# Patch gather by one-hot matmuls: f32 tables with a ScalarE selection, against bf16 parts with a VectorE comparison

## The chip, the cores and the metric

The kernel runs on one core of a Trainium2 chip. A core has five engines that run side by side, each through its own list of instructions in order: TensorE (PE, matmuls; PEld is its weight load), VectorE (DVE), ScalarE (ACT), GpSimd (POOL, here mostly an issuer of DMAs, with a few memsets) and SyncE (SP, DMA issue only). An engine waits where an instruction needs something that another engine or a DMA has not delivered yet. The metric is the device time of the core in microseconds.

## The reference

The input x has 8 images of 32 channels with 128 x 128 pixels. What is computed (normalisations `_gn`, two layers with residuals):

```python
def _patch_match_stack(x):           # for each pixel: the 8 of 25 offsets with the lowest 3x3-patch distance
    for dy in range(-2, 3):
        for dx in range(-2, 3):
            d = ((x - shifted(x, dy, dx)) ** 2).sum(1, keepdims=True)
            costs.append(conv(d, ones3x3, pad=1))
    _, idx = top_k(-cost, 8)
    g = x[:, yy(idx), xx(idx)]       # gather of the 8 shifted copies
    return g                         # [B, 32*8, H, W]

xb = _patch_match_stack(gn(x))
dct = conv(xb, dct_w, groups=32)
h = relu(depthwise3x3(conv1x1(xb, w1), w2))
h = relu(depthwise3x3(conv1x1(h, w3), w4))
wiener = sigmoid(depthwise3x3(conv1x1(h, w5), w6))
x = x + conv1x1(conv(wiener * dct, inv_dct_w, groups=32), agg_w)
x = x + conv5x5(gn(x), k5)           # per channel
```

## The kernel before

**Work on an image ahead of its use.** While the convolutions of image b run, the next image is prepared in small tasks: statistics and normalisation (`prep`), then `sources` and `squares`, `costs`, `places`. `squares` makes the differences to shifted copies on DVE (L421), squares them on ACT (L429) and sums over channels on PE (L436). `costs` sums patches on DVE, transposes on PE and takes the best 8 of 25 with MAX8 and FIND_INDEX8 on DVE (L513, L514). `places` turns offset numbers into places in a source table, transposes them on PE, and stores them as bf16 through POOL to `idxd` in HBM (L549).

**The source table.** `sources` transposes the normalised image on PE, four rows at a time (L390), copies it out on ACT (L392) and stores it through POOL to `xl` (L394). From `xl`, eighteen DMAs on POOL (L402, L406) build `xtd`: for each image row, 16 shifts and 11 pieces of 12 pixels (TW = 12, NT = 11), the 32 channels of the pixel in f32. A piece of 12 output pixels with offsets from -2 to 2 reaches QW = 16 source pixels, and four output rows reach 8 source rows, so 8 x 16 = 128 table rows: one for each partition.

**The gather.** A unit is half of the offsets (4 of 8) of four image rows; a step of eight rows has four units. `gather_load` fetches the table (`xt`, for every second unit) and two index tiles `ib`, each a row of HBM copied to all 128 partitions (L582). `gather_select` makes the one-hot on ACT: Square(ib - partition) in L596, Relu(1 - that) in L597, into `sel` in f32. `gather_pixels` runs one f32 matmul for each piece and offset: 32 columns of weights from `xt`, 48 columns (4 rows x 12 pixels) of `sel`, into one of four column groups of PE (L611); each f32 matmul is two instructions. ACT copies the result to `xb` (L618), and POOL stores `xb` to HBM (L620) for the final stage, which loads it again as `xf` (L769).

**The convolutions.** Three stages i = 1, 2, 3 each have a 1x1 convolution and a 3x3 depthwise one. Half of the channels goes the v way: PE (L649), ACT copy to `tv` (L657), then nine taps: the first on ACT (L700), eight on DVE (L703, scalar_tensor_tensor over 1024 elements), activation on ACT (L707). The other half goes the t way: PE (L673), ACT copy (L680), two copies by SP's DMAs, depthwise as matmuls on PE (L729), activation on ACT (L742). The final stage multiplies by the DCT on PE and DVE (L788, L796) and projects (L809, L817).

**Order.** The lists of PE, DVE and ACT are in program order. The main loop runs over steps of eight rows, with substeps i = 3, 2, 1, 0; i = 0 is the final stage. In each substep stand: the v matmuls of stage i; the image tasks of queues P and Q; half of the selection of unit u + 1; the loads of unit u + 3; `tick`, which takes image tasks for DVE up to a credit (estimated costs, summed in `total`); the eight taps; the t matmuls; the gather matmuls of unit u; the depthwise matmuls of the substep before; the A tasks (ACT); the other half of the selection. Before the loop, a prologue fills four units; `until` runs turns of image tasks (up to 4 us of DVE work each) until the index rows that a load needs are there (`ready`). In a turn each queue's tasks run once, so a chain of tasks that changes queues takes several turns.

Of the kernel before, what the change touches and what calls it, by code (L numbers as in the profile page):

```python
# [15 lines left out]
P = 128  # L16
# [4 lines left out]
NS = H // R  # L21
TW = 12
NT = 11
QW = TW + 4
HR = 38
HX = W + 4
SR = 6
EPS = 1e-5


# [12 lines left out]
def bm3d_conv_preact(  # L43
# [89 lines left out]
    nc.vector.tensor_copy(neg[:, 28:32], cst[:, C_B + 24 : C_B + 24 + P : 32])  # L133
    nplace = const.tile([P, 1], F32, name="nplace")
    nc.vector.tensor_scalar(nplace, cst[:, C_Q : C_Q + 1], -1.0, None, op0=ALU.mult)

# [245 lines left out]
    def sources(b, xn):  # L382


        xl = dram.tile([H, W, C], F32, name=f"xl_{b}", tag="xl")
        for r in range(0, 32, 4):
            yield "P", 0
            pt = ps_x.tile([P, 4, P], F32, name=f"px_{b}_{r}", tag="x")
            for q in range(4):
                nc.tensor.transpose(pt[:, q], xn[:, 3 + r + q, 2 : 2 + W], ident)  # L390
            xs = work.tile([P, 4, P], F32, name=f"xs_{b}_{r}", tag="ct")
            nc.scalar.copy(xs, pt)  # L392
            for q in range(4):
                nc.gpsimd.dma_start(  # L394
                    xl.rearrange("(g r) x c -> r x g c", g=4)[r + q],
                    xs[:, q].rearrange("p (g c) -> p g c", c=C),
                )
        xt = xtd[b] = dram.tile([H, QW, NT, C], F32, name=f"xtd_{b}", tag="xtd")
        for j in range(QW):
            ta, tz = (1 if j < 2 else 0), (NT if j < 10 else NT - 1)  # L400
            xa = TW * ta + j - 2
            nc.gpsimd.dma_start(  # L402
                xt[:, j, ta:tz], xl[:, xa : xa + TW * (tz - ta - 1) + 1 : TW]
            )
        for ja, jz, t, at in ((0, 2, 0, 0), (10, QW, NT - 1, W - 1)):
            nc.gpsimd.dma_start(  # L406
                xt[:, ja:jz, t], xl[:, at : at + 1].to_broadcast([H, jz - ja, C])
            )

# [109 lines left out]
    def places(b, idx, i):  # L519


        if i == 0:
            idxd[b] = dram.tile([4, 8, K * 4, W], BF16, name=f"idxd_{b}", tag="idxd")
        yield "D", 2.6
# [8 lines left out]
        for lim in (10.0, 15.0, 20.0):  # L533
# [5 lines left out]
            o3,  # L539
            cst[:, C_BASE : C_BASE + 4].unsqueeze(1).to_broadcast([P, 64, 4]),  # L540
            ALU.add,
        )
        yield "P", 0
        for h in range(2):
            pt = ps_x.tile([P, 512], F32, name=f"pi_{b}_{i}_{h}", tag="x")
            nc.tensor.transpose(pt[:, :P], o[:, h * P : (h + 1) * P], ident)
            li = work.tile([P, P], BF16, name=f"li_{b}_{i}_{h}", tag="li")
            nc.scalar.copy(li, pt[:, :P])
            nc.gpsimd.dma_start(  # L549
                idxd[b][2 * h : 2 * h + 2, 2 * i : 2 * i + 2].rearrange("g s k x -> g (s k) x"),  # L550
                li,
            )
        ready.add((b, i))
        if i == 3:
            ready.add(b)

    ready = set()
    xbs, xts, ibs, selss = {}, {}, {}, {}

    def gather_load(b, s4, g):  # L560

        if g == 0:

            xt = xts[b, s4] = work.tile([P, NT, C], F32, name=f"xt_{b}_{s4}", tag="xt", bufs=3)
            ys = [min(max(4 * s4 - 2 + r, 0), H - 1) for r in range(8)]
            if ys[7] - ys[0] == 7:
                nc.gpsimd.dma_start(
                    xt.rearrange("p t c -> p (t c)"),
                    xtd[b][ys[0] : ys[0] + 8].rearrange("r x t c -> (r x) (t c)"),
                )  # L570
            else:
                for r, y in enumerate(ys):
                    nc.gpsimd.dma_start(
                        xt[QW * r : QW * (r + 1)].rearrange("p t c -> p (t c)"),
                        xtd[b][y].rearrange("x t c -> x (t c)"),
                    )
        for k2 in range(2):
            ib = work.tile(
                [P, 2, 4, W], BF16, name=f"ib_{b}_{s4}_{g}_{k2}", tag="ib", bufs=5
            )  # L580
            k0 = 4 * g + 2 * k2
            nc.gpsimd.dma_start(  # L582
                ib.rearrange("p k y x -> p (k y x)"),
                idxd[b][s4 // 8, s4 % 8, 4 * k0 : 4 * k0 + 8]
                .rearrange("k x -> (k x)")
                .partition_broadcast(P),
            )
            ibs[b, s4, g, k2] = ib

    def gather_select(b, s4, g, k2=(0, 1)):  # L590
        for k2 in k2:
            sel = work.tile(
                [P, 2, 4, W], F32, name=f"sel_{b}_{s4}_{g}_{k2}", tag="sel", bufs=4
            )
            ib = ibs.pop((b, s4, g, k2))
            nc.scalar.activation(ib, ib, AF.Square, bias=nplace)  # L596
            nc.scalar.activation(sel, ib, AF.Relu, scale=-1.0, bias=1.0)  # L597
            selss[b, s4, g, k2] = sel

    def gather_pixels(b, s4, g):  # L600

        n, h = s4 // 2, s4 % 2
        if h == 0 and g == 0:
            xbs[b, n] = xbp.tile([P, 2, R, W], F32, name=f"xb_{b}_{n}", tag="xb")
        xb, xt = xbs[b, n], xts[b, s4]
        sels = [selss.pop((b, s4, g, k2)) for k2 in range(2)]
        pg = ps_x.tile([P, 4, W], F32, name=f"pg_{b}_{s4}_{g}", tag="x")
        for t in range(NT):
            xa, xz = TW * t, min(TW * (t + 1), W)
            for j in range(4):  # L610
                nc.tensor.matmul(  # L611
                    pg[C * j : C * (j + 1), :, xa:xz],
                    xt[:, t],
                    sels[j // 2][:, j % 2, :, xa:xz],
                    start=True,
                    stop=True,
                )
        nc.scalar.copy(xb[:, g, 4 * h : 4 * h + 4], pg)  # L618
        if h == 1 and g == 1:
            nc.gpsimd.dma_start(xbd[b][:, :, R * n : R * (n + 1)], xb)  # L620
# [305 lines left out]
    def middle(b, mr):  # L926
# [40 lines left out]
    units = [  # L967
        (b, 2 * n + h, g) if n < NS else None
        for b, n in steps
        for h in range(2)  # L970
        for g in range(2)
    ]
# [3 lines left out]
    def unit(stage, u, *rest):  # L976
        if 0 <= u < len(units) and units[u]:
            if stage is gather_load:
                at = (units[u][0], units[u][1] % 8 // 2)
                until(lambda: at in ready, 4.0)  # L980
            stage(*units[u], *rest)
# [9 lines left out]

    total = 5.5 + 3.3 + 36 * 1.95 + 4 * 4.6 + 32 * 1.85 + 4 * 2.6 + 4 * 3.6 + 6.6
    owed = [0.0]
# [19 lines left out]
    with tc.manual_schedule(engines=ORDERED):  # L1013
# [19 lines left out]
        for s in range(len(steps) + 2):  # L1033
# [10 lines left out]
            for i in (3, 2, 1, 0):  # L1044
# [22 lines left out]
                if s < len(steps):  # L1067
                    unit(gather_select, u + 1, (0,))
                    unit(gather_load, u + 3)
# [11 lines left out]
                if s < len(steps):  # L1081
                    unit(gather_select, u + 1, (1,))
                    u += 1
# [72 lines left out]
```

## Time and profile before

| what | us |
|---|---|
| median of three runs | 6811.16 |
| lowest and highest of them | 6809.01, 6819.06 |
| span of the profiled execution, first to last instruction | 6807.3 |
| mean granted clock of PE in it | 0.973 |

Some more groups of the same execution (count, busy us in total, mean ns of one):

| group | count | busy | mean |
|---|---|---|---|
| PE pg L611, 128x48 f32 | 40960 | 559.6 | 208 |
| PE pw L729 | 31680 | 2144.1 | 422 |
| PE px L390, transposes | 256 | 41.1 | 283 |
| ACT t L680, copies of 512 | 768 | 414.6 | 579 |
| ACT acc L707, activations of 1024 | 384 | 406.9 | 1060 |
| ACT xs L392, copies of 512 | 64 | 36.6 | 571 |
| DVE df L421 | 576 | 532.5 | 976 |
| POOL ib L582, DMA issue | 1024 | 570.7 | 558 |
| POOL idxd L549, DMA issue | 64 | 52.1 | 818 |
| POOL xl L394, DMA issue | 256 | 193.9 | 764 |
| POOL xtd L402, DMA issue | 128 | 127.3 | 1005 |

Matmuls are pipelined, so the mean of one is longer than the distance from one start to the next; busy is the time in which at least one of the group ran. DMA queues moved 1021.41 MB. The first gather matmul starts at 142 us, the first tap of L703 at 209 us, the last gather matmul at 6630.7 us.

### The profile page before, as it was taken

The numbers are of one execution on the slowest core, as the hardware profiler recorded it, in microseconds if no ns is written. First come the engines' busy times: TensorE is split into PE (matmuls) and PEld (weight loads), VectorE is DVE, ScalarE is ACT, GpSimd is POOL, SyncE is SP. The second block draws the span as 40 slices with busy tenths as digits, with TensorE's granted clock in tenths as the row PEclk, the third lists the DMA queues.
The fourth block names the chain that finished last, engine by engine and source line by source line (L and its number), as shares of the span: only waits on it lengthen the run. The fifth ranks groups of instructions, "written<-read, shape, count | busy, mean of one in ns | idle before, by whom it ended". The sixth has DMA issues, their size and how long they took to land.

```text
span 6807.3 us, 257036 instructions
## 1 busy us (share of the span) xinstructions
PE 6354.3 (93%) x113378; PEld 3352.8 (49%) x113378; DVE 5860.4 (86%) x8822; ACT 5064.6 (74%) x6698; POOL 3246.7 (48%) x5351
## 2 busy tenths in 40 slices
PE   5798899999999999999999999999999999999997
PEld 1454454554545455454554455545555454455553
DVE  7789988989889898898988888899888899877776
ACT  5787778777687777877777777877769777687772
POOL 7354446444464444544445444454436554344334
PEclk8899999999999999999999999999999999999998
DMA  4566656666566675666756656566665666566653
GB/s 90 143 153 153 151 149 154 159 152 158 147 156 155 144 169 135 163 151 152 167 135 158 161 146 169 138 165 159 149 150 151 162 156 152 138 170 157 154 151 80
DMA packets 809627, 1021.41 MB, mean 150 GB/s; under 512 B 255456, under 2 KB 619936, under 8 KB 808512
## 3 DMA queue, kind: packets, MB, share of 16 engines
q0 software_dynamic: 422432, 745.61, 42.9%
q1 hardware_dynamic: 383568, 258.11, 17.4%
q8 instruction: 892, 14.61, 0.9%
q10 hardware_dynamic: 2512, 1.25, 0.1%
q14 instruction: 223, 1.83, 0.1%
HBM read 553.25 MB, written 217.01 MB: 113 GB/s over the span
## 4 chain that ended last, share of the span: by engine, by line
PE 55%; DVE 23%; ACT 8%; DMA 6%; issue 5%; POOL 3%; SPq 0%; ACTq 0%; DVEq 0%; POOLq 0%
PE pw L729 18%; DVE acc L703 15%; PE pv L649 13%; PE p L673 12%; PE pg L611 4%; DVE df L421 3%; PE pc L788 2%; DMA t<-t 2%; PE p L902 2%; ACT df L429 2%; ACT ib L596 2%; DVE idx L514 1%; PE pa L809 1%; DMA xf<-xbd 1%; DVE acc L796 1%
## 5 line engine op out<-in xcount | busy, mean ns | idle before, releaser
L703 DVE SCALAR_TENSOR_TENSOR acc<-tv,dwv,acc 128x1024 f32<-128x1024 f32 (+3 forms) x3264 | 4032.9, 1237 | 249.6 <-ACT acc L700 140.3
L729 PE MATMUL pw<-t,dwd 96*32 96x254 f32 (+7 forms) x31680 | 2144.1, 422 | 84.7 <-issue 40.5
L729 PEld LDWEIGHTS pw<-t,dwd 96*32 96x32 f32 (+1 forms) x31680 | 1103.9, 111 | 906.6 <-issue 440.7
L582 POOL DMA_DIRECT2D ib<-idxd x1024 | 570.7, 558 | 1796.5 <-ACT sel L597 1620.6
L596 ACT ACTIVATE ib<-ib,nplace 128x1024 bf16<-128x1024 bf16 x1024 | 1170.1, 1143 | 9.5 <-DMA ib<-idxd 9.5
L597 ACT ACTIVATE sel<-ib 128x1024 f32<-128x1024 bf16 x1024 | 1084.8, 1059 | 32.5
L673 PE MATMUL p<-acc,lw 128*32 128x256 f32 x16768 | 989.1, 381 | 25.3 <-ACT tv L657 22.7
L649 PE MATMUL pv<-acc,lw 128*128 128x512 f32 (+1 forms) x2112 | 980.7, 607 | 29.9 <-DVE acc L796 27.4
L769 POOL DMA_DIRECT2D xf<-xbd x1088 | 650.2, 630 | 304.2 <-PE pc L788 87.0
L673 PEld LDWEIGHTS p<-acc,lw 128*32 128x32 f32 x16768 | 556.2, 111 | 454.9 <-ACT tv L657 62.5
L657 ACT COPY tv<-pv 128x512 f32<-128x512 f32 (+2 forms) x784 | 438.1, 578 | 390.4 <-PE pv L649 374.2
L611 PEld LDWEIGHTS pg<-sel,xt 128*32 128x32 f32 x45056 | 575.5, 111 | 252.1 <-issue 54.2
L429 ACT ACTIVATE df<-df 128x786 f32<-128x786 f32 (+2 forms) x576 | 468.0, 859 | 291.9 <-DVE df L421 289.2
L611 PE MATMUL pg<-sel,xt 128*32 128x48 f32 x45056 | 592.7, 207 | 80.4 <-ACT sel L597 46.0
L421 DVE TENSOR_TENSOR df<-xn 128x786 f32<-128x786 f32 (+2 forms) x576 | 532.5, 976 | 116.0 <-PE pd L436 109.2
L742 ACT ACTIVATE acc<-pw 128x512 f32<-128x512 f32 (+2 forms) x808 | 439.9, 573 | 249.7 <-PE pw L729 249.0
L649 PEld LDWEIGHTS pv<-acc,lw 128*128 128x128 f32 x2112 | 384.2, 193 | 475.6 <-issue 398.1
L707 ACT ACTIVATE acc<-acc 128x1024 f32<-128x1024 f32 (+3 forms) x408 | 416.8, 1022 | 229.7 <-DVE acc L703 229.5
L680 ACT COPY t<-p 128x512 f32<-128x512 f32 x800 | 424.6, 570 | 127.7 <-PE p L673 125.7
L700 ACT ACTIVATE acc<-tv,dwv 128x1024 f32<-128x1024 f32 (+3 forms) x408 | 454.5, 1114 | 52.6 <-PE pa L809 35.0
L649 PE MATMUL pv<-xb,lw 128*128 128x512 f32 x1024 | 477.4, 609 | 0.0
L673 PE MATMUL p<-xb,lw 128*32 128x256 f32 x8192 | 468.1, 380 | 4.4 <-DVE xy L914 4.4
(151 smaller groups left out, 5782.5 us busy)
## 6 DMA issues: line engine op xcount, KB each, us to landing
ib<-idxd POOLq DMA_DIRECT2D x1024, 256.0 KB, 4.4
xbd<-xb POOLq DMA_DIRECT2D x128, 1024.0 KB, 6.7
xf<-xbd POOLq DMA_DIRECT2D x960, 128.0 KB, 7.3
t<-t SPq DMA_DIRECT2D x792, 128.0 KB
t<-t SPq DMA_DIRECT2D x384, 256.0 KB
tv<-tv SPq DMA_DIRECT2D x384, 130.0 KB
xt<-xtd POOLq DMA_DIRECT2D x240, 176.0 KB, 4.6
xl<-xs POOLq DMA_DIRECT2D x256, 64.0 KB, 2.6
```

Source lines behind the costliest of these rows:

```text
L421: nc.vector.tensor_sub(df[:, :, ca:cz], xn[:, r0 : r0 + SR, ca:cz], xn[:, r0 + dy : r0 + dy + SR, ca + dx : cz + dx],)
L429: nc.scalar.activation(df[:, :, ca:cz], df[:, :, ca:cz], AF.Square)
L582: nc.gpsimd.dma_start(ib.rearrange("p k y x -> p (k y x)"), idxd[b][s4 // 8, s4 % 8, 4 * k0 : 4 * k0 + 8] .rearrange("k x -> (k x)") .part ...
L596: nc.scalar.activation(ib, ib, AF.Square, bias=nplace)
L597: nc.scalar.activation(sel, ib, AF.Relu, scale=-1.0, bias=1.0)
L611: nc.tensor.matmul(pg[C * j : C * (j + 1), :, xa:xz], xt[:, t], sels[j // 2][:, j % 2, :, xa:xz], start=True, stop=True,)
L649: nc.tensor.matmul(ps[:, :hr], lhsT[:, g, P:CK], src(g)[:, h : h + hr], start=g == 0, stop=g == 1,)
L673: nc.tensor.matmul(ps[C * r : C * (r + 1), e, :nb], lhsT[:, g, s], rows[:, r : r + 4 * nb - 3 : 4], start=g == 0, stop=g == 1,)
L700: nc.scalar.activation(acc, rows, AF.Copy, scale=tap)
L703: nc.vector.scalar_tensor_tensor(acc, rows, tap, acc, op0=ALU.mult, op1=ALU.add)
L729: nc.tensor.matmul(pt[u][C * j : C * (j + 1), ka:kz, :nb, xa:xz], dwd[0:hi, i - 1, u, j, dx + 1], t[0:hi, j, ka:kz, :nb, xa + dx : xz + dx ...
L769: nc.gpsimd.dma_start(xf[p : p + C, m, j0:j1], src[g, m, (h + m + 1) % 2, :, :, ya:yz])
```

## The change

The table holds each pixel in three bf16 parts (the value rounded to bf16, the rest rounded, and the rest of that), 96 values in place of 32 f32. The parts are made from the normalised image: a copy to bf16 on ACT, a subtraction on DVE, again a copy and a subtraction; then each part is transposed as bf16. Three matmuls per piece and offset, one for each part, sum in PSUM. Pieces are 11 pixels, QW = 15, so 8 x 15 = 120 table rows; they start anew at column 64, six for each half. A unit is now all 8 offsets of four rows in one half of the columns, with one index tile of 2048 bf16. The one-hot is one comparison on DVE, in place, with the partition number. A matmul takes two offsets at once: 2 x 4 x 11 = 88 columns. `places` adds a base by half, and its result is stored in twice as many DMAs. A load also waits until the source table of its image is complete (`sourced`).

```diff
-TW = 12
-NT = 11
+TW = 11
+NT = 12
+HW = W // 2
+NP = 3
...
     def sources(b, xn):
-        xl = dram.tile([H, W, C], F32, name=f"xl_{b}", tag="xl")
+        xl = dram.tile([H, W, NP * C], BF16, name=f"xl_{b}", tag="xl")
         for r in range(0, 32, 4):
-            yield "P", 0
-            pt = ps_x.tile([P, 4, P], F32, name=f"px_{b}_{r}", tag="x")
-            for q in range(4):
-                nc.tensor.transpose(pt[:, q], xn[:, 3 + r + q, 2 : 2 + W], ident)
-            xs = work.tile([P, 4, P], F32, name=f"xs_{b}_{r}", tag="ct")
-            nc.scalar.copy(xs, pt)
-            for q in range(4):
+            rows = xn[:, 3 + r : 7 + r, 2 : 2 + W]
+            yield "A", 0
...
+            nc.scalar.copy(parts[0], rows)
+            yield "D", 0.7
+            nc.vector.tensor_sub(rest, rows, parts[0])
+            yield "A", 0
+            nc.scalar.copy(parts[1], rest)
+            yield "D", 0.7
+            nc.vector.tensor_sub(parts[2], rest, parts[1])
+            for q0 in (0, 2):
+                yield "P", 0
+                pt = ps_x.tile([P, 2, 4, NP, C], BF16, name=f"px_{b}_{r}_{q0}", tag="x")
+                for q in range(2):
+                    for s in range(NP):
+                        nc.tensor.transpose(pt[:, q, :, s], parts[s][:, q0 + q], ident_b)
+                xs = work.tile([P, 2, 4, NP * C], BF16, name=f"xs_{b}_{r}_{q0}", tag="xs")
+                nc.scalar.copy(xs, pt.rearrange("p q g s c -> p q g (s c)"))
+                for q in range(2):
+                    nc.gpsimd.dma_start(
+                        xl.rearrange("(g r) x e -> r x g e", g=4)[r + q0 + q], xs[:, q]
+                    )
+        xt = xtd[b] = dram.tile([H, QW, NT, NP * C], BF16, name=f"xtd_{b}", tag="xtd")
+        for j in range(QW):
+            for f in range(2):
...
                 nc.gpsimd.dma_start(
+                    xt[:, j, ta:tz], xl[:, xa : xa + TW * (tz - ta - 1) + 1 : TW]
+                )
...
+        sourced.add(b)
...
     def gather_load(b, s4, f):
...
-        for k2 in range(2):
-            ib = work.tile([P, 2, 4, W], BF16, name=f"ib_{b}_{s4}_{g}_{k2}", tag="ib", bufs=5)
...
+        ib = work.tile([P, K, 4, HW], BF16, name=f"ib_{b}_{s4}_{f}", tag="sel", bufs=4)
+        nc.gpsimd.dma_start(
+            ib.rearrange("p k y x -> p (k y x)"),
+            idxd[b][s4 % 8 // 2, s4 // 8 * 2 + s4 % 2, f].rearrange("k x -> (k x)").partition_broadcast(P),
+        )
...
-            nc.scalar.activation(ib, ib, AF.Square, bias=nplace)
-            nc.scalar.activation(sel, ib, AF.Relu, scale=-1.0, bias=1.0)
+    def gather_select(b, s4, f):
+        ib = ibs[b, s4, f]
+        nc.vector.tensor_scalar(ib, ib, place, None, op0=ALU.is_equal)
...
-        for t in range(NT):
-            xa, xz = TW * t, min(TW * (t + 1), W)
-            for j in range(4):
-                nc.tensor.matmul(
-                    pg[C * j : C * (j + 1), :, xa:xz],
-                    xt[:, t],
-                    sels[j // 2][:, j % 2, :, xa:xz],
-                    start=True,
-                    stop=True,
-                )
-        nc.scalar.copy(xb[:, g, 4 * h : 4 * h + 4], pg)
+        for t in range(NT // 2):
+            xa, xz = TW * t, min(TW * (t + 1), HW)
+            for s in range(NP):
+                for j in range(4):
+                    nc.tensor.matmul(
+                        pg[C * j : C * (j + 1), :, :, xa:xz],
+                        xt[: 8 * QW, f * (NT // 2) + t, C * s : C * (s + 1)],
+                        sel[: 8 * QW, j : j + 5 : 4, :, xa:xz],
+                        start=s == 0,
+                        stop=s == NP - 1,
+                        skip_group_check=True,
+                    )
+        nc.scalar.copy(xb[:, :, 4 * h : 4 * h + 4, HW * f : HW * (f + 1)], pg)
...
-                until(lambda: at in ready, 4.0)
+                until(lambda: at in ready and at[0] in sourced, 4.0)
...
-    total = 5.5 + 3.3 + 36 * 1.95 + 4 * 4.6 + 32 * 1.85 + 4 * 2.6 + 4 * 3.6 + 6.6
+    total = 5.5 + 3.3 + 8 * 1.4 + 36 * 1.95 + 4 * 4.6 + 32 * 1.85 + 4 * 2.6 + 4 * 3.6 + 6.6
...
-                    unit(gather_select, u + 1, (0,))
+                    unit(gather_select, u + 1)
                     unit(gather_load, u + 3)
                     tick(b, i)
...
-                    unit(gather_select, u + 1, (1,))
                     u += 1
```

## The prediction

> **What bounds the kernel now.** I read the engine totals first, then the engines' busy time by stretches of the span, then the groups of instructions by form, then the waits, and last the order in time of a few stretches.
>
> The engine totals give busy time and its share of the span: PE is nearly full, DVE is second.
>
> ```profile
> PE 6354.3 (93%) x113378; PEld 3352.8 (49%) x113378; DVE 5860.4 (86%) x8822; ACT 5064.6 (74%) x6698; POOL 3246.7 (48%) x5351
> ```
>
> The stretches (start:end, length, then busy us of PE, PEld, DVE, ACT, POOL) say where each is the limit.
>
> ```profile
> 0.00:210.00 210.00, 100.94 (x964) 38.14 (x968) 146.31 (x427) 109.19 (x153) 145.67 (x214) 0.76 0.44 98
> 210.00:580.00 370.00, 348.13 (x6398) 187.82 (x6390) 325.94 (x456) 304.03 (x399) 167.91 (x272) 0.98 0.62 154
> 580.00:830.00 250.00, 222.80 (x4120) 121.43 (x4122) 238.71 (x471) 186.76 (x246) 107.54 (x189) 0.97 0.63 148
> 830.00:5750.00 4920.00, 4690.63 (x84224) 2481.32 (x84220) 4337.01 (x6522) 3755.78 (x4973) 2400.79 (x3961) 0.98 0.63 154
> 5750.00:6650.00 900.00, 881.58 (x16448) 470.68 (x16444) 709.36 (x789) 673.17 (x868) 356.92 (x622) 0.99 0.61 153
> ```
>
> From 830 to 5750 us PE is busy 4691/4920 = 95.3%, DVE 88.2%. In the last image, where no next image is prepared, PE reaches 98.0% with DVE at 78.8%. From 580 to 830 us it is the other way round: DVE 95.5%, PE 89.1%, and there the chain of waits names DVE's taps (27%) first. So DVE's work is already a limit wherever it exceeds some 95% of the time.
>
> By form (count, busy us, mean ns of one):
>
> ```profile
> L703 DVE SCALAR_TENSOR_TENSOR acc<-tv,dwv,acc 128x1024 f32<-128x1024 f32 x3072 | 3940.6, 1284 | 232.4 <-ACT acc L700 130.7 <-PE p L673 4.6 <-DMA tv<-tv 0.9
> L596 ACT ACTIVATE ib<-ib,nplace 128x1024 bf16<-128x1024 bf16 x1024 | 1170.1, 1143 | 9.5 <-DMA ib<-idxd 9.5
> L597 ACT ACTIVATE sel<-ib 128x1024 f32<-128x1024 bf16 x1024 | 1084.8, 1059 | 32.5
> L796 DVE TENSOR_TENSOR acc<-acc,pc 128x512 f32<-128x512 f32 x496 | 308.5, 681 | 55.4 <-PE pc L788 55.4
> L532 DVE TENSOR_SCALAR oc<-oc 128x256 f32<-128x256 f32 x32 | 9.7, 302 | 1.1
> L367 DVE TENSOR_SCALAR xn<-xn,mr_a 128x5016 f32<-128x5016 f32 x8 | 23.6, 2952 | 0.4
> ```
>
> In time order, one gather unit and the depthwise matmuls behind it (start, length, tiles, count):
>
> ```profile
> 3035.49 1.09 PE L611 MATMUL pg<-sel,xt 128*32 128x48 f32 x88
> ...
> 3036.40 5.35 PE L729 MATMUL pw<-t,dwd 96*32 96x256 f32 x96
> ```
>
> **The change, part by part.**
>
> *ACT.* 1024 pairs of Square and Relu go: 1024 x (1.143 + 1.059) = 2255 us. Added are 128 copies of 512 elements (0.58 us, as the copies of L680) and 128 of 768 (0.8, between the 0.58 of 512 elements and L707's 1.06 of 1024) in place of 64 of 512 (0.57): 74 + 102 - 37 = +139. ACT falls from 5065 to about 2949 us, 43%. ACT was not the limit, so this pays only through waits: in 830 to 5750 us little of DVE's and PE's idle time names ACT's selection (PE at L611 about 25 us). I book nothing for it separately.
>
> *PE, the gather.* Before, a unit has 44 f32 matmuls, each issued as two instructions, hence 88 at 1.10/88 = 12.5 ns each, four column groups side by side. The depthwise row gives 5.35/96 = 55.7 ns for 256 columns. Slope: (55.7 - 12.5)/(256 - 48) = 0.208 ns a column, with 2.5 ns fixed. After, a unit has 6 x 3 x 4 = 72 bf16 instructions of 88 columns (72 in the last piece). No bf16 matmul is in the trace. Upper end: a column costs what it costs in an f32 pass, 2.5 + 88 x 0.208 = 20.8 ns, 1.50 us a unit. Lower end: columns cost nothing and only the 2.5 ns stay, 0.18 us. I take half the slope, because an f32 element has twice the bytes: 11.7 ns, 0.84 us. Then 512 x 0.26 = 133 us leave PE. The value is nearer to the 12.5 ns row than either end is. The Trainium skill (TensorE: Matmul & The Clock Gate, section Wait — 56ns, not 53.3ns?) puts a floor of about 25 ns under the start-to-start of small matmuls; by it a unit would take 72 x 25 = 1.80 us and PE would gain 358 us of work. The row above, 12.5 ns across four column groups, speaks against that floor here, and the measurement decides.
>
> *PE, the source transposes.* 256 instructions (0.66 us for four, 41 us in all) become 768 of bf16; at half the time each 61 us, at the same time each 123. I take +20. PE: 6354 - 133 + 20 = 6241 us.
>
> *DVE, the comparison.* 512 instructions of 2048 bf16 elements, in place. No bf16 instruction of DVE is in the trace. The two TENSOR_SCALAR rows give (2952 - 302)/(5016 - 256) = 0.557 ns an element, half of what the two-input rows take ((1284 - 681)/512 = 1.18). Either way two f32 inputs are read in some 1.1 to 1.2 ns, which I read as a limit by bytes. Upper end, f32 rate: 0.302 + 1792 x 0.557 = 1.30 us. Lower end: the 256-element row alone, 0.30 us. By bytes: 0.302 + 1792 x 0.279 = 0.80 us; less the overlap of neighbours I take 0.78, or 399 us in all. The Trainium skill (VectorE: DVE Perf Modes, section The perf-mode tier table) gives 693 ns for a bf16 tensor_scalar of 2048 elements in SBUF; by it the sum would be 355 us, and no row here shows it.
>
> *DVE, the split.* 128 subtractions of 512 elements at 0.68 (the L796 row): 87 us. DVE: 5860 + 399 + 87 = 6346 us, now above PE.
>
> *Order on DVE.* The comparison of the next unit stands ahead of the queued image work and of the eight taps. It waits for its index load, issued two units (some 24 us) earlier and landing in 4.4 us; ACT's idle time before the same data was 9.5 us in the whole run. So the wait costs nothing while the load keeps that lead; if POOL is late, the taps behind it are late, then ACT's activation and PE's next stage.
>
> *POOL and DMA.* Index loads go from 1024 to 512 issues (-286 us of issuing), index stores from 64 to 128 (+52), xtd stores from 18 to 32 an image, a burst of 24 to 32 us where it was 17.5. Ahead of the burst's end nothing of POOL moves: row stores and xf loads behind it come some 10 us later. In the trace the burst at 1142.67 us left PE busy 19.9 of 20 us, so I charge nothing, with 5 us an image (35) as the high side. SP's queue is untouched. Table loads grow from 176 to 270 KB, with xl and xtd about 4% more traffic, at a DMA share of 0.63.
>
> *Start.* The source table now takes a chain of copy, subtraction, copy, subtraction, transposes per group of four rows, and no gather load starts before it is complete. In the instruction order, the first comparison comes after 120 of image 0's 128 sorts, and the last split about 20 us of DVE work before it. DVE from 30 us on: 72 differences (67 us), sorts (51), cost sums (21), places (9), splits (11), the rest 2 and 8 idle: 199 us. The last split is thus at about 180, then 8 for transposes and stores, 28 for the xtd burst, 4 landing, 8 to load the table: first gather at 228, against 142. Before, 67 us pass from there to the first tap, spent on sorting the next band; after, that is done, and 20 should do: 250 against 209. Cost +40, between +10 and +80, with 16 us of image work done early.
>
> *Sum.* From 210 to 5750 us lie 5540/6489 of the gather, 437 units, and 112 splits. DVE: 326 + 239 + 4337 + 437 x 0.78 + 76 - 16 = 5303 us. The best long stretch ran DVE at 95.5% with PE at 89%; here PE wants 93% at the same time, and ACT is freer. I take 95%: 5303/0.95 = 5582, +42. The last image is PE's: 71 x 0.26 = -18. Profiled execution: 6807.3 + 42 + 40 - 18 = 6871; the median of the runs is 3.9 above its span, so 6875.
>
> **Rivals.** *DVE keeps up, faster.* PE has the least slack today, and with ACT at 43% DVE rarely waits; single stretches of 47.8 us show DVE at 97.8%. Then PE sets 210 to 5750: (5262 - 114 + 17)/0.953 = 5420, -120, and the time is 6811 - 120 + 40 - 18 = 6713. It decides once DVE sustains over 95.7% (5303/5540). Against it: 250 us at 95.5% were DVE's best, with PE starved.
>
> *The comparison runs at the f32 rate.* 437 x 0.52 = 227 us more on DVE: 5530/0.95 = 5821, +281: 7114. For it: ACT's L596 shows that bf16 gains nothing there. Against it: the byte reading of DVE's two rates.
>
> *bf16 passes are no faster a column.* PE gains 437 x 0.40: 5262 + 175 + 17 = 5454, /0.953 = 5723, +183, and +28 in the last image: 7062.
>
> *Gains and costs cancel:* no change, where DVE sustains about 96 to 96.5% and the longer start takes back what is won.
>
> **How the numbers follow.** DVE as the new limit, with its own range of 6820 to 6990: 0.50. DVE keeps up: 0.30. No change: 0.07. The two slow prices together: 0.13. About 0.2% (14 us) is what a measurement of this kernel can tell from none. Faster 0.30, same 0.07, slower 0.63. The range goes from the faster rival's 6713, a little lower for a cheaper gather, to the dear comparison: 6700 to 7110, leaving about 0.1 outside on each side.
>
> **What would show it.** Right: DVE near 6350 us and 92% of the span, comparison near 0.78 us, a gather unit near 0.84 us, ACT near 43%; PE's share below DVE's from 830 to 5750 us; first tap near 250 us. Wrong: DVE over 96% there with the time under 6797; a comparison of 1.3 us; a unit above 1.1 us; or a first tap near 209 us.

## The result and the profile after

The changed kernel takes 6915.1 us (median of four runs, 6881.8 to 6937.1) against 6810.3 us for the kernel before: a ratio of 1.015, interval 1.0124 to 1.0177. It is slower by 105 us, where 64 were forecast. Its profiled execution took 6913.75 us, with a span of 6912.0.

The engine totals of the changed kernel (busy us, share of the span, instructions):

```profile
PE 6365.5 (92%) x105698; PEld 3262.0 (47%) x105698; DVE 6275.3 (91%) x9466; ACT 3196.6 (46%) x4842; POOL 3131.2 (45%) x5015
```

ACT has lost 1868 us, DVE has gained 415, and PE, which was to lose over 100, has gained 11. The same stretches as before (start:end, length, then busy us of PE, PEld, DVE, ACT, POOL, the granted clock, the DMA share and GB/s):

```profile
0.00:210.00 210.00, 84.91 (x444) 28.27 (x444) 164.54 (x498) 92.33 (x141) 133.52 (x193) 0.74 0.34 75
210.00:580.00 370.00, 333.67 (x6022) 178.59 (x6022) 318.61 (x387) 181.91 (x269) 129.44 (x217) 0.94 0.63 160
580.00:830.00 250.00, 217.61 (x3514) 109.41 (x3518) 242.36 (x492) 115.51 (x177) 110.45 (x187) 0.93 0.55 140
830.00:5750.00 4920.00, 4640.44 (x77560) 2379.41 (x77556) 4585.71 (x6854) 2337.16 (x3547) 2279.41 (x3654) 0.97 0.64 159
5750.00:6650.00 900.00, 872.30 (x15156) 457.55 (x15152) 776.29 (x997) 387.31 (x582) 375.91 (x610) 0.99 0.66 165
```

From 830 to 5750 us DVE went from 88.2% to 93.2% and PE from 95.3% to 94.3%. The chain of waits, by engine and by line, moved the same way. Before, PE had 55% of it and DVE 23%, with the depthwise matmuls first:

```profile
PE 55%; DVE 23%; ACT 8%; DMA 6%; issue 5%; POOL 3%; SPq 0%; ACTq 0%; DVEq 0%; POOLq 0%
PE pw L729 18%; DVE acc L703 15%; PE pv L649 13%; PE p L673 12%; PE pg L611 4%; DVE df L421 3%; PE pc L788 2%; DMA t<-t 2%; PE p L902 2%; ACT df L429 2%; ACT ib L596 2%; DVE idx L514 1%; PE pa L809 1%; DMA xf<-xbd 1%; DVE acc L796 1%
```

After:

```profile
PE 45%; DVE 35%; DMA 8%; issue 4%; POOL 3%; ACT 2%; SPq 0%; DVEq 0%; ACTq 0%; POOLq 0%
DVE acc L734 22%; PE pw L760 14%; PE pv L680 11%; PE p L704 10%; PE pg L641 3%; DMA t<-t 3%; DVE df L459 3%; PE pc L819 2%; DVE idx L552 2%; DVE ib L627 2%; DVE acc L827 2%; PE pd L474 2%; DMA xf<-xbd 1%; PE pa L840 1%; PE p L933 1%
```

DVE's taps now head the chain, and L627, the new comparison, has 2% of its own. Its line alone (duration min/median/max in ns, first and last start in us):

```profile
L627 DVE TENSOR_SCALAR ib<-ib,cst x512: 723/749/1161, 197.4 to 6725.4; 128x2048 bf16<-128x2048 bf16 x171
```

One gather unit in order of time (start, length, tiles, count), and then, from the groups by form, the bf16 transposes and the second of the two new subtractions (count, busy us, mean ns of one):

```profile
3019.28 1.00 PE L641 MATMUL pg<-ib,xt 120*32 120x88 bf16 x72
```

```profile
L422 PE MATMUL px<-ident_b,part 128*128 128x128 bf16 x768 | 68.9, 227 | 14.7 <-DVE part L416 7.3 <-ACT part L414 7.1 <-ACT part L410 0.2
...
L416 DVE TENSOR_TENSOR part<-rest,part 128x512 bf16<-128x512 f32 x64 | 43.5, 679 | 0.7 <-ACT part L414 0.7
```

A unit's 72 instructions take 1.00 us, which divided by 72 is 13.9 ns; before, 88 took 1.09 to 1.12 us. Both lengths hold the time that the last instruction itself takes, some 0.2 us, as the lines of the two groups show (duration min/median/max in ns; before, then after):

```profile
L611 PE MATMUL pg<-sel,xt x45056: 190/206/289, 142.1 to 6630.7; 128*32 128x48 f32 x181, 128*32 128x32 f32 x19
L641 PE MATMUL pg<-ib,xt x36864: 197/207/288, 224.0 to 6735.8; 120*32 120x88 bf16 x169, 120*32 120x72 bf16 x31
```

From start to start it is (1.00 - 0.207)/71 = 11.2 ns after and (1.09 - 0.206)/87 = 10.2 ns before. The taps start at 248.7 us instead of 209.0, the gather at 224.0 instead of 142.1.

Where the 105 us arise shows when the same instruction is followed through the traces. DVE's instructions that write acc come in the same number, 3792 (474 an image), in every kernel here. The table, worked out from the traces, gives how many us later than in the kernel before the k-th of them starts. The columns other than "after" are experiments that follow ("compare+1" has the comparison's price doubled).

```
k              after  no compare  quick start  compare+1  transposes only
1                 40          40           22         42               40
360               41          24           35         74               35
474 (1 image)     61          35           46         93               36
1896 (4)          79          15           81        223               13
3318 (7)         113          10          121        358               -7
3792 (all)       105          -7          114        351              -21
```

So the start costs 40 us (39.7 at the first, which is the first tap of L734), the rest of the first seven images, while a later table is made, adds another 74, and the last image gives 8 back.

### The profile page after: what moved, and what is told of

The parts are those of the page before. It is cut to its first block, busy times and chain, and to the rows that moved or that the text cites. A ratio compares the mean times of both kernels' runs of the same rounds, so it can differ in the third digit from the quotient of the medians.

```text
span 6912.0 us, 239783 instructions
## 1 busy us (share of the span) xinstructions
PE 6365.5 (92%) x105698; PEld 3262.0 (47%) x105698; DVE 6275.3 (91%) x9466; ACT 3196.6 (46%) x4842; POOL 3131.2 (45%) x5015
## 4 chain that ended last, share of the span: by engine, by line
PE 45%; DVE 35%; DMA 8%; issue 4%; POOL 3%; ACT 2%; SPq 0%; DVEq 0%; ACTq 0%; POOLq 0%
DVE acc L734 22%; PE pw L760 14%; PE pv L680 11%; PE p L704 10%; PE pg L641 3%; DMA t<-t 3%; DVE df L459 3%; PE pc L819 2%; DVE idx L552 2%; DVE ib L627 2%; DVE acc L827 2%; PE pd L474 2%; DMA xf<-xbd 1%; PE pa L840 1%; PE p L933 1%
## 5 line engine op out<-in xcount | busy, mean ns | idle before, releaser
L734 DVE SCALAR_TENSOR_TENSOR acc<-tv,dwv,acc 128x1024 f32<-128x1024 f32 (+3 forms) x3264 | 4036.2, 1237 | 189.7 <-ACT acc L731 84.5
L760 PEld LDWEIGHTS pw<-t,dwd 96*32 96x32 f32 (+1 forms) x31680 | 1054.1, 111 | 996.3 <-issue 525.5
L680 PE MATMUL pv<-acc,lw 128*128 128x512 f32 (+1 forms) x2112 | 972.8, 603 | 39.1 <-DVE acc L827 34.6
L711 ACT COPY t<-p 128x512 f32<-128x512 f32 x800 | 460.9, 579 | 723.4 <-PE p L704 703.1
L619 POOL DMA_DIRECT2D ib<-idxd x512 | 292.5, 572 | 941.6 <-PE pg L641 775.4
L680 PEld LDWEIGHTS pv<-acc,lw 128*128 128x128 f32 x2112 | 380.6, 191 | 484.6 <-issue 382.4
L641 PEld LDWEIGHTS <-xt 120*32 120x32 bf16 x36864 | 504.2, 99 | 216.2 <-issue 112.0
L641 PE MATMUL pg<-ib,xt 120*32 120x88 bf16 (+1 forms) x36864 | 537.4, 213 | 45.1 <-DMA xt<-xtd 31.4
L738 ACT ACTIVATE acc<-acc 128x1024 f32<-128x1024 f32 (+3 forms) x408 | 414.6, 1016 | 296.5 <-DVE acc L734 296.3
L649 ACT COPY xb<-pg 128x512 f32<-128x512 f32 x512 | 300.0, 586 | 498.4 <-PE pg L641 497.9
L426 POOL DMA_DIRECT2D xl<-xs x256 | 200.3, 786 | 621.2 <-ACT xs L424 446.8
L731 ACT ACTIVATE acc<-tv,dwv 128x1024 f32<-128x1024 f32 (+3 forms) x408 | 454.7, 1114 | 57.5 <-PE pa L840 44.4
L680 PE MATMUL pv<-xb,lw 128*128 128x512 f32 x1024 | 477.9, 610 | 0.0
```

What stands on the lines that cost most here:

```text
L641: nc.tensor.matmul(pg[C * j : C * (j + 1), :, :, xa:xz], xt[: 8 * QW, f * (NT // 2) + t, C * s : C * (s + 1)], sel[: 8 * QW, j : j + 5 : 4 ...
L680: nc.tensor.matmul(ps[:, :hr], lhsT[:, g, P:CK], src(g)[:, h : h + hr], start=g == 0, stop=g == 1,)
L711: nc.scalar.copy(t[: C * nr, 2 * q : 2 * q + 2, 2 : 2 + nb], ps[: C * nr, :, :nb])
L731: nc.scalar.activation(acc, rows, AF.Copy, scale=tap)
L734: nc.vector.scalar_tensor_tensor(acc, rows, tap, acc, op0=ALU.mult, op1=ALU.add)
L760: nc.tensor.matmul(pt[u][C * j : C * (j + 1), ka:kz, :nb, xa:xz], dwd[0:hi, i - 1, u, j, dx + 1], t[0:hi, j, ka:kz, :nb, xa + dx : xz + dx ...
```

## The experiments

All are changes to the kernel after, but for the one named as a change to the kernel before. Every ratio is to the kernel before. Differences between two variants carry some ±25 us, from the widths of their two intervals.

**The comparison left out.**

```diff
     def gather_select(b, s4, f):
         ib = ibs[b, s4, f]
-        nc.vector.tensor_scalar(ib, ib, place, None, op0=ALU.is_equal)
+        pass
```

> The changed kernel without the comparison on VectorE (the index tile goes into the matmuls as it is, so the gathered pixels are not the reference's). Theory A, VectorE's extra work is what lengthens the loop: DVE falls by some 380 us to about 5890, and the time to about 6840 (before plus the longer start of 40 us, less 10 for the freer ScalarE). Theory B, the loss is on PE (slower gather than hoped, more transposes, lower granted clock) or in POOL's longer table burst: the time stays above 6890.

6758.7 us, ratio 0.9913, interval 0.9884 to 0.9942: below the values of both theories. Its profiled run was the longest of four (6800.0 us):

```profile
PE 6326.3 (93%) x105698; PEld 3269.0 (48%) x105698; DVE 5938.9 (87%) x8954; ACT 3204.5 (47%) x4842; POOL 3078.4 (45%) x5015
```

The comparison costs 156 us of time for 383 us of instructions (512 x the median of 0.749) and 336 us of DVE's busy time (6275 - 5939; the rest of an instruction overlaps with its neighbours). The rest is hidden: without it PE is the fuller engine. Everything else that the change brings, start, tables and ACT's relief included, leaves the kernel 52 us below the one before.

**The one-hot back on ACT, all else as after.** Square and Relu, in place in bf16.

```diff
+    nplace = const.tile([P, 1], F32, name="nplace")
+    nc.vector.tensor_scalar(nplace, place, -1.0, None, op0=ALU.mult)
...
-    def gather_select(b, s4, f):
-        ib = ibs[b, s4, f]
-        nc.vector.tensor_scalar(ib, ib, place, None, op0=ALU.is_equal)
+    def gather_select(b, s4, f, k2=(0, 1)):
+        for k in k2:
+            ib = ibs[b, s4, f][:, 4 * k : 4 * k + 4]
+            nc.scalar.activation(ib, ib, AF.Square, bias=nplace)
+            nc.scalar.activation(ib, ib, AF.Relu, scale=-1.0, bias=1.0)
...
-                    unit(gather_select, u + 1)
+                    unit(gather_select, u + 1, (0,))
...
+                    unit(gather_select, u + 1, (1,))
```

> The changed kernel with the one-hot made on ScalarE again by Square and Relu, in bf16 and in place, in two halves at the old places of the order. ScalarE goes back to about 79% of the span, VectorE to about 5890 us. Theory A: as without the comparison, about 6840. Rival: ScalarE's freedom was worth something, then it comes out 30 us or more above the run without the comparison. If the bf16 gather is worth its 50 us of PE, it can fall below 6811 only by what the longer start does not take.

6907.0 us, ratio 1.014, interval 1.0123 to 1.0156: the same as with the comparison on DVE.

```profile
PE 6366.2 (92%) x105698; PEld 3299.1 (48%) x105698; DVE 5940.2 (86%) x8955; ACT 5192.0 (75%) x6890; POOL 3081.2 (45%) x5015
```

No engine is over 92% here, and ACT, which got the work, is at 75%; yet against no one-hot at all it costs 6907 - 6759 = 148 us. The waits of PE (us in all, times, longest) show only a third of that directly; the other lines are waits for ACT's other products:

```profile
PE pi L586 <- DVE oc L577: 60.0, 18, 10.4
...
PE pd L476 <- ACT df L469: 51.1, 45, 7.9
PE pg L645 <- ACT ib L631: 50.3, 30, 3.6
```

The waits that name an engine thus show only part of what its work costs. By this, the kernel before was paying a price of about this size on ACT, and the change replaces it by one of the same size on DVE; the kernel before was not run without its one-hot, so for it the price is inferred.

**A quick start.** Image 0's table is made in one turn for each row group, without giving way to other work in between.

```diff
-            yield "D", 0.7
+            if b:
+                yield "D", 0.7
...
-                yield "P", 0
+                if b or not q0:
+                    yield "P", 0
```

> The changed kernel with the source table of image 0 made in one turn per row group (copies, subtractions and transposes follow each other without turns between). First tap at 210 to 230 us instead of 249. Theory A with the start priced at 40: 6875 to 6895. Rival: the work done early in the longer start comes back into the loop, and the time stays within 10 us of 6915.

6916.7 us, ratio 1.0156, interval 1.0139 to 1.0173: nothing gained, though the gather starts at 174.5 us (after: 224.0) and the taps at 230.8 (248.7). The table above shows that the head start is lost on the way: at the first of the counted instructions this variant is 22 us behind the kernel before (after: 40), at the 474th 46 (61), and at the 1896th 81 (79). What takes the 18 us back, and which of image 0's work makes up the 40 us, stays open.

**The comparison's price doubled.** Another bf16 instruction of the same size ahead of each comparison.

```diff
         ib = ibs[b, s4, f]
+        nc.vector.tensor_scalar(ib, ib, 1.0, None, op0=ALU.mult)
         nc.vector.tensor_scalar(ib, ib, place, None, op0=ALU.is_equal)
```

> The changed kernel with a second VectorE instruction of the same size ahead of each comparison (the index tile times 1.0, in place; the result is the same). Without the comparison the time was 6759, with it 6915: 156 us for 383 us of VectorE, 0.41 of its length. Theory A, VectorE is now the limit of the loop: a second 383 us shows with a larger share, 0.6 to 0.9, so 7140 to 7260. Rival, PE and VectorE share the limit as before: 0.4 again, near 7070. Rival B, VectorE still has room: under 7000.

7161.5 us, ratio 1.0508, interval 1.048 to 1.0537.

```profile
PE 6430.9 (90%) x105698; PEld 3293.2 (46%) x105698; DVE 6633.7 (93%) x9978; ACT 3196.3 (45%) x4842; POOL 3173.6 (44%) x5015
```

The second instruction costs 246 us where the first cost 156: here the price of one more instruction grew with what DVE already had. (A second comparison into a tile of its own was tried first and gave no time: the tile did not fit into the on-chip memory beside the others.)

**Two matmuls instead of three a piece and offset.** The third part is left out of the sum; the table holds it still.

```diff
-            for s in range(NP):
+            for s in range(2):
...
-                        stop=s == NP - 1,
+                        stop=s == 1,
```

> The changed kernel with the third bf16 part left out of the gather matmuls (48 in place of 72 a unit; the pixels are exact to two parts only). PE loses 24 x 13.9 ns x 512 = 171 us of work. Theory A, VectorE is the limit: less than 40 us shows, 6875 to 6915. Rival, PE still counts as much: 80 to 170 us show, 6745 to 6835.

6892.6 us, ratio 1.0112, interval 1.0083 to 1.0141.

```profile
PE 6253.0 (91%) x93410; PEld 3133.2 (45%) x93410; DVE 6274.7 (91%) x9466; ACT 3171.3 (46%) x4842; POOL 3124.0 (45%) x5015
```

The time falls by 22 us, no more than the runs of one kernel differ. DVE's share stays at 91.0%. A unit of the gather in this variant:

```profile
3008.63 0.73 PE L641 MATMUL pg<-ib,xt 120*32 120x88 bf16 x48
```

So the work taken away is 512 x (1.00 - 0.73) = 138 us; the 171 of the expectation comes from 13.9 ns an instruction, which counts in the last one's own length. In the changed kernel a third of the gather's matmuls is all but free, and PE's 92% does not make it the limit. PE's busy time fell by 112 us, less than the 138: the granted clock of this execution is lower too, 0.954 against 0.962, and matmuls at the lower clock are busy for longer (last section; by the estimate there, 34 us of it).

**The first image's table used for all**, in the kernel after and in the kernel before. Tables of images 1 to 7 are neither made nor stored, and their pixels come from image 0; the table's 8 x 1.4 us go out of the planner's total. The edit below is that of the kernel after; the kernel before has no `sourced`, and its total no such term.

```diff
     def sources(b, xn):
+        if b:
+            xtd[b] = xtd[0]
+            sourced.add(b)
+            return
```

> The changed kernel with the source table of image 0 used for all images: for images 1 to 7 no split, no transposes, no stores to xl and xtd (the pixels of these images come from the wrong image). Taken away are 7/8 of 87 us on VectorE, of 175 us on ScalarE, of the PE transposes and of POOL's table bursts. Theory C, the table's making is a part of the loss as large as the comparison: 6915 falls by 60 us or more. Theory A with the comparison alone: it falls by what 76 us of VectorE are worth at 0.4, 30 us, to about 6885.

> The kernel before with the source table of image 0 used for all images in the same way (the pixels of images 1 to 7 come from the wrong image). Its table costs no VectorE work, so under theory A it falls by less than 20 us, to 6790 or more; if POOL's bursts and PE's transposes cost by themselves, by 30 us or more. The difference between the fall of the changed kernel and this one is what the new table costs more than the old.

After: 6790.8 us, ratio 0.997, interval 0.9956 to 0.9983. Before: 6752.1 us, ratio 0.9911, interval 0.9884 to 0.9938. Seven tables cost 124 us in the changed kernel (6915.1 - 6790.8) and 58 in the old one (6810.3 - 6752.1, or 60 by the runs taken beside it): the new table is about 65 us dearer. The 39 us between these two variants are the later start: followed as in the table above, the variant of the kernel after lies 39 us behind that of the kernel before at the first of the counted instructions, 40 at the 1896th and 45 at the 3318th. So without later tables the new gather, comparison and all, comes out even with the old one, and the 105 us are start and tables.

**Which part of the table?** Three variants take the later tables apart. The first and the third also drop the table's 8 x 1.4 us from the planner's total, the second keeps them; what that is worth by itself was not run. First, only the split goes: all three parts are the first one, its transposes and stores stay.

```diff
-                for s in range(NP)
+                for s in range(1 if b else NP)
...
+            if b:
+                parts = [parts[0]] * NP
+            else:
...
                 nc.vector.tensor_sub(parts[2], rest, parts[1])
```

> The changed kernel where, for images 1 to 7, the split is left out: all three parts are the first one (no subtractions on VectorE, one ScalarE copy less for each row group; pixels of these images are three times the bf16 value). Transposes, stores and table bursts stay. Of the 124 us that one table for all images saved, theory D (the VectorE work of the table counts): 40 to 90 us fall away, 6825 to 6875. Theory P (POOL's and the DMAs' work counts): under 40, 6875 to 6915.

6901.1 us, ratio 1.0135, interval 1.0112 to 1.0158: a gain of 14 us, though DVE does 71 us less. DVE's waits from 830 to 5850 us of this variant, and then of the kernel after, tell what took its place:

```profile
DVE xr L851 <- PE pa L843: 97.5, 33, 7.3
DVE ib L630 <- DMA ib<-idxd: 87.8, 6, 15.1
```

```profile
DVE xr L848 <- PE pa L840: 101.0, 34, 10.0
DVE acc L734 <- ACT acc L731: 47.2, 60, 4.3
DVE acc L827 <- PE pc L819: 25.1, 23, 4.8
DVE tmp_a L243 <- ACT tmp_a L266: 21.1, 6, 7.9
DVE ib L627 <- DMA ib<-idxd: 13.6, 1, 13.6
```

The comparison now stands waiting for its index load, 88 us in six waits, instead of once for 13.6. In the trace each of the six waits is for a load that POOL issued 6 to 9 us behind a table's burst of 32 `xtd` stores, 5 to 9 us ahead of its comparison, where the lead is 30 us in the median; the taps stand behind the comparison. The burst lasts 26 us in both kernels, while the stores to `xl` ahead of it take 197 us an image here and some 600 after. Why the burst meets such a load in six images here and in one after is not shown. The next variant takes the stores away and not the waits alone. It keeps the split, the transposes and the copies of every image, and leaves out the stores of images 1 to 7.

```diff
-                for q in range(2):
+                for q in range(0 if b else 2):
...
+        if b:
+            xtd[b] = xtd[0]
+            sourced.add(b)
+            return
```

> The changed kernel where, for images 1 to 7, split, transposes and copies are made, but nothing is stored to xl and xtd (448 DMA issues, 350 us of POOL, fewer; the table of image 0 serves all). Theory P: 50 to 100 us fall away, 6815 to 6865. Theory D: under 40, 6875 to 6915.

6877.2 us, ratio 1.0118, interval 1.009 to 1.0145: the stores cost 38 us, with the ±25 of such a difference, and theory P's 50 us at least did not come. DVE's wait for index loads, over the whole run, is the start's and little else, as its longest shows:

```profile
DVE ib L631 <- DMA ib<-idxd: 34.1, 3, 31.6
```

Then both edits together, so that only the first copy, the transposes and the PSUM copies of a later table are left:

> The changed kernel where, for images 1 to 7, only the first bf16 copy, the transposes and the copies out of PSUM are made; no split, no stores (the table of image 0 serves all). Full table 6915, without split 6901, without stores 6877, nothing at all 6791. If the parts add up: 6915 - 14 - 38 = 6863, so that transposes and copies are worth 72 us. If the three parts only cost together (any one alone is hidden): 6791 to 6820.

6785.4 us, ratio 0.9951, interval 0.9932 to 0.9969, the same as with no later table at all (6790.8). The totals without stores, and then without stores and split:

```profile
PE 6339.0 (92%) x105698; PEld 3256.0 (47%) x105698; DVE 6270.5 (91%) x9466; ACT 3195.1 (47%) x4842; POOL 2754.9 (40%) x4567
```

```profile
PE 6300.9 (93%) x105698; PEld 3251.8 (48%) x105698; DVE 6202.3 (91%) x9354; ACT 3164.9 (47%) x4786; POOL 2756.1 (41%) x4567
```

With the stores gone, taking away 68 us of split on DVE saves 92 us; with the stores there it saved 14, for the comparison then waited. In the totals without stores and split, and in those without later tables (DVE 6201.0 us in a span of 6774.7), DVE is at 91.4 and 91.5%, as after (90.8), with two matmuls (91.0) and without stores (91.3): in all of these the time is DVE's work divided by about 0.912. Without the split alone, where the comparison waits, it is 90.0%.

**Half the one-hots on each engine.** Every second unit's one-hot is made by ACT, as above.

```diff
+        if f == 0:
+            if 0 in k2:
+                ib = ibs[b, s4, f]
+                nc.vector.tensor_scalar(ib, ib, place, None, op0=ALU.is_equal)
+            return
```

> The changed kernel with every second unit's one-hot made on ScalarE (Square, Relu in bf16, in two halves at the old places) and the others by the comparison on VectorE. With none the time was 6759, all on VectorE 6915, all on ScalarE 6907. If the two engines' prices add in proportion: 6911. If each engine's price grows with its load, as the second VectorE instruction cost 246 us after 156 for the first: 6820 to 6880. Below 6811 it would beat the kernel before.

6854.6 us, ratio 1.0066, interval 1.0042 to 1.0089. All on DVE took 6915, all on ACT 6907: shared, it is 56 us below the middle of the two.

```profile
PE 6339.0 (93%) x105698; PEld 3282.7 (48%) x105698; DVE 6106.5 (89%) x9211; ACT 4185.7 (61%) x5866; POOL 3102.2 (45%) x5015
```

It is the fastest variant that computes all of the reference, and slower than the kernel before.

**The same with two parts throughout.** The third part is left out of the table, the split and the matmuls, so pixels keep two bf16 parts.

```diff
-NP = 3
+NP = 2
...
-            nc.vector.tensor_sub(rest, rows, parts[0])
-            yield "A", 0
-            nc.scalar.copy(parts[1], rest)
-            yield "D", 0.7
-            nc.vector.tensor_sub(parts[2], rest, parts[1])
+            nc.vector.tensor_sub(parts[1], rows, parts[0])
```

The planner's total has 8 x 0.7 us for it, and the one-hots are shared as in the variant before.

> Two bf16 parts in place of three throughout (the third part of each pixel is left out, so pixels are kept to two bf16 parts), and every second unit's one-hot on ScalarE as in the run with half of them there. From its 6855: a third fewer gather matmuls (22 us with VectorE as the limit, more where it is not), a third fewer transposes and table bytes, half the subtractions. If all limits are shared: 6770 to 6810, at or below the kernel before. If VectorE alone decides: 6830 to 6850.

6795.5 us, ratio 0.9966, interval 0.9953 to 0.9979: 20 us below the runs of the kernel before beside it, with less of the computation done. Of all variants that make their own tables and their one-hots it is the only one ahead of the kernel before.

## Why the prediction was right, and where it was off

**The limit and the sign.** The likeliest case, DVE as the new limit, is what came: removing DVE's work pays (92 us for 68), adding it costs (246 for 383), and 138 us less on PE pay 22. The rival in which DVE keeps up asked for over 95.7% of the stretch; 93.2% is what the trace shows from 830 to 5750 us.

**The comparison.** 0.749 us against 0.78: the time that the reading of DVE's two f32 rates as a limit by bytes gave is what came, and the rival at f32 rate (1.30 us) is out. In busy time each adds only 336/512 = 0.66 us, less than the 0.78 that I took with the overlap of neighbours in it. The Trainium skill's VectorE: DVE Perf Modes (The perf-mode tier table) gives 693 ns, and the row's 749 ns lies 8% above it.

**DVE's 95%, the mis-sized term.** By 0.66 us a unit, 437 x 0.12 = 52 us less work lay on DVE than in my 5303: 5251 us, which at 95% would have made 5527 us, 13 less than before. Those seven images took some 74 us more (from +40 at the first tap to +113), 5614 us, so DVE ran at 93.5%; the trace has DVE busy 5243.7 of the 5615 us from 250 to 5865, 93.4%. The share was taken from the best 250 us of the old trace, and the whole loop did not reach it. The two errors, -55 and +87, with 10 us that the last image did not give back, make up the 41 us between 64 and 105 to within one. That the sum came no further off is in part luck, for the two large ones have opposite signs.

**ACT, "I book nothing for it separately".** The step fails. It was argued from the small idle time that named ACT's selection, 25 us at L611; the one-hot on ACT costs 148 us with ACT at 75%. The sum did not visibly suffer, because it divides DVE's work by one share, in which ACT's relief and PE's are hidden. That is luck more than reasoning: the share came from a stretch in which ACT still made the one-hot.

**PE, the gather.** The pace was about right and the saving was not. From start to start the instructions are 11.2 ns apart, near my 11.7. But my 12.5 ns for the old ones came from dividing the whole length of the row, 1.10 us, with the last instruction's own 0.2 us in it, and the 0.84 us for the new unit leave that out. The old ones are 10.2 ns apart, and a unit falls from 1.09 to 1.00 us: 512 x (1.09 - 1.00) = 46 us leave PE, not 133. Since PE is not the limit this moved the time little (138 us of it were worth 22). The floor of about 25 ns in the Trainium skill's TensorE: Matmul & The Clock Gate (Wait — 56ns, not 53.3ns?) is not what this row shows: with four column groups side by side the instructions follow each other at 11.2 ns. Transposes rose by 28 us (41.1 to 68.9) against the +20 taken, and cost no time that can be seen: with the transposes of later tables (6785.4 us) the kernel is no slower than without them (6790.8).

**PE's share below DVE's from 830 to 5750 us: wrong.** It is 94.3% to DVE's 93.2%. PE's busy time also holds the matmuls that ran at half clock after a wait, which I had not counted (last section), so the shares can't tell which of two nearly full engines sets the pace. The experiments could.

**The burst, "I charge nothing".** The step fails: the table's stores cost 38 us in all (±25), about the high side of 35; part of it was there before, as seven old tables cost 58 to 60 with theirs. The queue that I had named, the comparison behind a late index load and the taps behind it, is what the variant without the split shows (87.8 us).

**The start.** The gather at 224.0 and the taps at 248.7 us, against 228 and 250: +40 as forecast. That the delay is paid to the end is what the two kernels without later tables show, 39 us apart. That an earlier table is the cure is not shown: the quick start gained nothing.

**The last image.** -8 against -18.

## What to carry over

An engine at 75% was not free here, and one at 86% had no 14% to give. Several engines run in order and wait for each other; moving work from one to another traded one price for a similar one, and sharing it was 52 to 60 us better than either. Find the price of a piece of work by taking it out on either side, not from the idle time that names it, and expect the next piece on the same engine to cost more (156, then 246 us). Look at what stands ahead of a load on its queue when an in-order engine waits for it: removing 71 us of other work gained 14, while the waits behind late loads grew by 74. And when a row's length is divided by its count, take the last instruction's own time out first, on both sides of the comparison.

## What the hardware showed that I had not expected

- A bf16 comparison on DVE in place, 2048 elements against a value for each partition, takes 0.749 us in the median, 0.37 ns an element with the fixed part. In the variant with the price doubled, the multiplication of the same tile by a constant took 0.699 us in the mean, the comparison behind it 0.777. ACT's Square of 1024 bf16 elements took 1.143 us; its f32 rows of that size take 1.05 (L738) and 1.15 (L731).
- Within a unit of the gather, at full clock, the matmuls follow each other at 10.8 ns for 88 columns and 9.3 for 72 (bf16, 120 rows), and before at 10.8 for 48 columns and 7.0 for 32 (f32, 128 rows); these are medians over the traces (with its pauses, the unit shown above averages 11.2). So a column costs 0.12 to 0.13 ns in bf16 and 0.22 in f32, a little more than half. Three bf16 parts still save little, because a unit now streams 6144 columns where it streamed 4096 (2048 f32 columns, each in two instructions).
- The clock granted to TensorE is full or half, and a half stretch lengthens the matmuls in it. One of the changed kernel (the stretch, with the clock as the third number from the end, then PE's first rows in it, with the idle time ahead in brackets):

```profile
2966.20:2976.30 10.10, 5.47 (x102) 2.68 (x106) 8.52 (x11) 1.09 (x2) 2.28 (x4) 0.50 0.35 80
2970.83 1.98 PE L819 MATMUL pc<-xf,ldct 64*64 64x512 f32 x6 [6.86 <-DVE acc L827]
2972.74 1.59 PE L641 MATMUL pg<-ib,xt 120*32 120x88 bf16 x72
```

PE had waited 6.86 us for DVE, and the gather unit takes 1.59 us instead of 1.00. Over a whole trace, matmuls of 512 columns (L680) start 853 ns apart in such stretches and 429 elsewhere. PE was busy for 75% at most of the 5 us ahead of any of them (95% on average from 260 us on before, 94% after). From 260 us on, the kernel before has 45 of them, 249 us with PE busy in 177; the changed kernel 71, 381 us and 290; the variant with two matmuls 83, 492 us and 358. If half of that busy time is extra, the clock adds 145 us to PE's busy time after and 89 before: an estimate of 56 us more, enough to explain that PE's busy time rose by 11 us although the gather took 46 less and the transposes 28 more. How much of it reaches the 105 us stays open. The mean clock does not order the variants: it went from 0.973 to 0.962 with the change, and the variant with two parts and shared one-hots had 0.959 and was below the kernel before.

- Runs of the changed kernel differ by 0.8% (6881.8 to 6937.1 us), the runs of the kernel before taken with them by 0.15%. The shortest of the changed kernel had the highest clock (0.965), the longest one of the lowest (0.962), and of the thirteen later runs of the kernel before the shortest (6793.0 us) had 0.979 and the longest (6829.9) 0.974. Which is the cause and which the effect no run here tells.
